# Half of a tile's edge messages added in pairs by VectorE, row scatters moved to the end of a step: a graph layer and an expert layer in one stream

## The chip, the cores and the metric

The kernel runs on one core of one Trainium2 chip. The metric is device time in microseconds of one launch, the median of several runs. A profile of one further execution gives the engines' instructions: PE is TensorE, DVE VectorE, ACT ScalarE, POOL GpSimd, SP SyncE. L12 is line 12 of the kernel.

## The reference, cut to what matters

Four layers on 6250 nodes with 256 features and 100000 edges: a first graph layer, a first expert layer, and then the two that matter here, a graph attention layer (4 heads of 64) and a layer of 8 experts, of which each node takes two.

```python
# third layer, x normalised per row
h = (x @ W).reshape(n, HEADS, OUT_C)
a_src = einsum('nhc,hc->nh', h, att_src); a_dst = einsum('nhc,hc->nh', h, att_dst)
e = a_src[src] + a_dst[dst]                 # edges, and a loop at each node
e = where(e > 0, e, 0.2 * e)
ex = exp(e - segment_max(e, dst)[dst])
alpha = ex / (segment_sum(ex, dst)[dst] + 1e-16)
out = segment_sum(alpha[:, :, None] * h[src], dst)
x = x + relu(out.reshape(n, 256) + bias)
# fourth layer, xf = x normalised again
gate_logits = xf @ Wg + bg                  # 8 experts
top_w, top_i = top_k(gate_logits, 2); top_w = softmax(top_w)
x = x + sum over the two experts e of top_w * (gelu(xf @ W1[e] + b1[e]) @ W2[e] + b2[e])
```

## The kernel before

Nodes are sorted by degree, so that a tile of 128 nodes has nodes of like degree; 49 tiles, and CAPS[t] is the number K of edge slots that tile t has (41, then 25 down to 8; 813 in all). A table in HBM holds for each node its row of h with its attention terms and, in the second half, x.

The third and fourth layers run as one stream (ffn1, from L1421), a loop of steps written out by hand: each engine runs its instructions in the order in which the program issues them. In step s

- POOL gathers tile s (gather, L1223): one indirect DMA for the tile's own rows (L1229), and one for each of its K slots (L1239), 128 rows each. The slots lie in one to four chunks of up to 13 slots, in buffers g of which there are five. After each gather the program calls between(), which issues one instruction from a list, the outbox, if there is one.
- DVE works on tile s-1 (q1): scores (L1247) and, after an exponential on ACT, shares (L1265), which writes the weights into PSUM. messages (L1276) multiplies the gathered rows of a chunk by their weights, in place (L1284). total (L1286) sums them over the slots on PE: one matmul with the identity for each slot, accumulated in PSUM (L1293; the fp32 matmul counts as two in the profile).
- Tile s-2 (q2) is finished: result (L1295) adds bias, relu and x, the row is normalised (L1547), turned by PE (L1550), and PE computes its gate logits (L1447). DVE adds the gate bias into sc (L1583).
- When a group of mostly four tiles has its logits, choose (L697), count (L732, on PE), place (L740) and listed (L793) find for each row its two experts and its two places in the experts' lists, and written (L825) has PE turn the list of full blocks (L830). The rows are then scattered to the experts' table, one indirect DMA of POOL for each tile and choice (scatters, L761; L768): for a group of four tiles 8 of them go into the outbox for the next step. Their offsets are the slots that place computes; the profile shows that wait under L802, an instruction of DVE just behind.
- One block of 256 rows is put through its expert per step, in three stages over three steps: rows and weights are fetched by SP (fetch, L1450, with xr at L844, which waits for the scatters of its round; fetch2, L1457); inner (L1463, matmuls L1470, gelu L1474); outer (L1476, L1481); and finish (L897, L899) on DVE. ACT normalises the fetched rows (L1489).

PE's order in a step is: outer, the turn of tile s-2, inner, the turn of the new block's rows, gate, total of chunk 0, count, total of the other chunks, written. DVE's order is: scores, result and normalisation, shares, messages of chunk 0, finish, choose, gate bias, places, messages of the other chunks, place and listed. Tiles come mostly in order of rising K, tile 0 with K = 41 in step 8. After the last tile the remaining blocks go through their experts alone, and the two parts of the output are added.

Of the kernel before, what the change touches and what calls it, by code (L numbers as in the profile page):

```python
# [27 lines left out]
CAPS = [41, 25, 24, 23, 22, 21, 21, 20, 20, 20, 19, 19, 19, 18, 18, 18, 18, 18, 17, 17, 17, 17, 16, 16,  # L28
        16, 16, 16, 15, 15, 15, 15, 15, 14, 14, 14, 14, 14, 13, 13, 13, 12, 12, 12, 12, 11, 11, 10, 9, 8]
# [6 lines left out]
def gnn_moe_kernel(ctx: ExitStack, tc: tile.TileContext, a: dict, out: bass.AP):  # L36
    nc = tc.nc
    x, src, dst = a["x"], a["src"], a["dst"]
    N, D = x.shape
# [28 lines left out]
    ident = keep.tile([P, P], F32, name="ident")  # L68
# [1207 lines left out]
    def messages(q, c):  # L1276

        al, own = q["al"], q["own"]
        if c == 0:
            hv = own[:, :D].rearrange("p (h c) -> p h c", h=H)  # L1280
            nc.vector.tensor_mul(hv, hv, al[:, q["K"], :, None].to_broadcast([P, H, C]))
        g, k0, m = q["gs"][c]
        gv = g[:, :m, :D].rearrange("p k (h c) -> p k h c", h=H)
        nc.vector.tensor_mul(gv, gv, al[:, k0 : k0 + m, :, None].to_broadcast([P, m, H, C]))  # L1284

    def total(sums, q, c):  # L1286

        po = sums[:, q["half"], :]
        if c == 0:
            nc.tensor.matmul(po, ident, q["own"][:, :D], start=True, stop=False)  # L1290
        g, k0, m = q["gs"][c]
        for k in range(m):
            nc.tensor.matmul(po, ident, g[:, k, :D], start=False, stop=k0 + k == q["K"] - 1)  # L1293

    def result(pool, sums, bias_b, q, x3):  # L1295
        y = pool.tile([P, D], F32, name="att_y")
# [124 lines left out]
    def ffn1(tab, bias_b):  # L1421
        NX, _, HD = a["L1_ffn_W1"].shape
        NM = HD // P
        with tc.tile_pool(name="f1", bufs=1) as fp, tc.tile_pool(name="f1r", bufs=2) as rp, \
# [7 lines left out]
            bg = fp.tile([P, NX], F32, name="bg")  # L1432
# [5 lines left out]
            with tc.tile_pool(name="f1p", bufs=2, space=PSUM) as psum:  # L1438
# [5 lines left out]
                def gate(xT):  # L1444
                    pl = small[:, 256 : 256 + NX]
                    for k in range(2):
                        nc.tensor.matmul(pl[:, :NX], xT[:, k, :], wg[:, k, :], start=(k == 0), stop=(k == 1))  # L1447
                    return pl
# [47 lines left out]
                seq = []  # L1496
                rows_in = 0
                for g, n in parts:
                    grp = dict(g=g, n=n, last=(g, n) == parts[-1], pad=g + n == NT)
# [9 lines left out]
                outbox, sends, coming, kept = [], [], [], []  # L1509
# [9 lines left out]
                s = 0  # L1519
                while s < len(seq) or ready or new or cur or prev or q1 or q2 or group or outbox or coming or kept:  # L1520
# [11 lines left out]
                    if q2 is not None:  # L1532
                        grp, i = q2["grp"], q2["i"]
# [22 lines left out]
                    if n_c:  # L1556
                        messages(q1, 0)
# [19 lines left out]
                    if q2 is not None:  # L1577
                        pl = gate(xT)
                    if group is not None:
                        st = moe.choose(rp, group["g"], group["n"], group["rw"], group["sc"], group["pad"])  # L1580
                        moe.weigh(st)
                    if q2 is not None:
                        nc.vector.tensor_add(grp["sc"][:, i, :], pl[:, :NX], bg)  # L1583
                    if n_c:
                        total(sums, q1, 0)
                    if group is not None:
# [4 lines left out]
                    for c in range(1, n_c):  # L1591
                        messages(q1, c)
                        total(sums, q1, c)
                    if group is not None:
                        slot = moe.place(rp, st)
                        moe.listed(rp, group["last"])
                        moe.compare(group["due"], group["last"])
                        li = moe.written(rp, psum)
                        if group["last"]:
                            nc.vector.tensor_copy(list_i, li)  # L1600
                            moe.left(left_i)

                    def between():
                        if outbox:
                            outbox.pop(0)()

                    q0 = None
                    if s < len(seq):
                        grp0, i0, end0 = seq[s]
                        q0 = gather(ap_, tab, grp0["g"] + i0, between)  # L1610
                        q0.update(grp=grp0, i=i0, end=end0, half=s % 2)
                    while outbox:
                        nc.gpsimd.memset(gap, 0.0)
                        between()
                    ready, coming = ready + coming, []
                    outbox, sends = sends, []
                    if group is not None:
# [6 lines left out]
                    q1, q2 = q0, q1  # L1624
# [3 lines left out]
        with tc.tile_pool(name="f1o", bufs=8) as op_, \  # L1628
# [21 lines left out]
            while ys:  # L1650
                g, n, k, y = ys.pop(0)
# [69 lines left out]
    with tc.tile_pool(name="order", bufs=1) as order_pool, \  # L1721
            tc.tile_pool(name="order_ps", bufs=1, space=PSUM) as order_psum:
        with tc.manual_schedule(engines={ET.SP, ET.PE, ET.Activation, ET.DVE, ET.Pool}), \
                tc.tile_pool(name="g1w", bufs=1) as g1w:
            with tc.tile_pool(name="f0", bufs=1) as fp:
                k0 = {"g1w": g1w}
# [7 lines left out]
    nc.vector.tensor_scalar_mul(bias_b, bias_b, fast)  # L1734
    whole.__exit__(None, None, None)
    ffn1(tab, bias_b)


# [27 lines left out]
```

## Time and profile before

| | us |
| --- | --- |
| median of 3 runs | 2492.31 (2491.33 to 2493.85) |
| profiled execution: own time | 2483.9 |
| profiled execution: span | 2482.2 |
| busy: PE / DVE / ACT / POOL | 1848.9 / 1219.9 / 941.8 / 1498.1 |
| first and last gather of the stream (L1239) start at | 828.6 and 2079.2 |
| last matmul of the experts (L1481) begins in the group at | 2409.99 |
| mean granted TensorE clock | 0.87 of full |

The span runs from the first to the last instruction. "issue" is idle time in which the engine waited for nothing that the profile shows. A group of instructions is shown with its line, engine, operation, output and inputs, its count, its busy time in us and the mean of one in ns, and the idle time of its engine just before it with what ended most of that. In a timeline the columns are the start in us, the duration in us, the engine, the line, and in brackets the idle time before with what ended it. Busy time of an engine alone does not say what bounds the kernel: PE, for instance, waits inside the stream while the sum of its work is the largest.

### The profile page before, as it was taken

The numbers are of one execution on the slowest core, as the hardware profiler recorded it, in microseconds if no ns is written. First come the engines' busy times: TensorE is split into PE (matmuls) and PEld (weight loads), VectorE is DVE, ScalarE is ACT, GpSimd is POOL, SyncE is SP. The second block draws the span as 40 slices with busy tenths as digits, with TensorE's granted clock in tenths as the row PEclk, the third lists the DMA queues.
The fourth block names the chain that finished last, engine by engine and source line by source line (L and its number), as shares of the span: only waits on it lengthen the run. The fifth ranks groups of instructions, "written<-read, shape, count | busy, mean of one in ns | idle before, by whom it ended". The sixth has DMA issues, their size and how long they took to land.

```text
span 2482.2 us, 31090 instructions
## 1 busy us (share of the span) xinstructions
PE 1848.9 (74%) x8343; PEld 1544.8 (62%) x8344; DVE 1219.9 (49%) x4459; ACT 941.8 (38%) x1967; POOL 1498.1 (60%) x1778
## 2 busy tenths in 40 slices
PE   4743758887967463549589898988989796799990
PEld 3522646676855342438478787777877676678880
DVE  3668765562328453455455564554646364311112
ACT  3754545553437220124234343343334232244330
POOL 3557357767545577676776767677777775234430
PEclk8955878898989776669899999999999998899995
DMA  7514345678869543355667667666766664387748
GB/s 215 122 40 132 108 140 169 198 222 236 255 201 297 134 115 104 99 175 156 209 206 223 205 192 220 214 204 203 237 200 201 198 199 157 115 290 262 266 170 312
DMA packets 346252, 471.68 MB, mean 190 GB/s; under 512 B 70206, under 2 KB 283237, under 8 KB 346071
## 3 DMA queue, kind: packets, MB, share of 16 engines
q1 hardware_dynamic: 261868, 272.15, 35.0%
q0 software_dynamic: 72112, 186.44, 25.4%
q10 hardware_dynamic: 12090, 11.03, 1.3%
q8 instruction: 69, 1.13, 0.2%
q14 instruction: 113, 0.92, 0.1%
HBM read 374.44 MB, written 95.02 MB: 189 GB/s over the span
## 4 chain that ended last, share of the span: by engine, by line
PE 33%; POOL 15%; DMA 7%; issue 7%; ACT 6%; DVE 5%; SPq 1%; DVEq 0%; POOLq 0%; ACTq 0%
POOL g L1239 11%; PE ph L1470 10%; PE py L1481 10%; PE sums L1293 7%; DMA g<-t_d,idx 3%; POOL idx L253 2%; PE ph L1038 2%; DMA yg<-f_parts 2%; DMA idx<-src_d,start_i 1%; POOL f_rows L768 1%; ACT L1474 1%; ACT L402 1%; ACT hT L1474 1%; ACT bxn L1489 1%; ACT L1263 1%
## 5 line engine op out<-in xcount | busy, mean ns | idle before, releaser
L1239 POOL DMA_INDIRECT g<-t_d,idx x813 | 776.4, 955 | 248.6 <-issue 228.2
L1470 PE MATMUL ph<-bxT,w 128*128 128x256 f32 x1728 | 411.4, 395 | 29.7 <-ACT hT L1474 29.7
L1470 PEld LDWEIGHTS ph<-bxT,w 128*128 128x128 f32 x1728 | 337.8, 199 | 90.7 <-ACT hT L1474 43.8
L1293 PE MATMUL sums<-g,ident 128*128 128x256 f32 x1626 | 387.5, 398 | 2.8 <-DVE g L1284 2.8
L1481 PE MATMUL py<-w,hT 128*128 128x256 f32 x1728 | 386.0, 382 | 2.0 <-DMA w<-in_L_ffn_W 2.0
L1293 PEld LDWEIGHTS sums<-g,ident 128*128 128x128 f32 x1626 | 323.8, 201 | 59.9 <-DVE g L1284 12.4
L1481 PEld LDWEIGHTS py<-w,hT 128*128 128x128 f32 x1728 | 329.3, 192 | 47.0 <-DMA w<-in_L_ffn_W 2.3
L768 POOL DMA_INDIRECT f_rows<-rw,slot x196 | 197.9, 1010 | 134.3 <-DVE ci L802 71.6
L1284 DVE TENSOR_TENSOR g<-g,weights 128x2048 f32<-128x2048 f32 (+6 forms) x88 | 229.5, 2610 | 0.0
L1474 ACT ACTIVATE hT<-ph,bcol 128x256 f32<-128x256 f32 x432 | 177.3, 471 | 136.5 <-PE ph L1470 131.1
L897 DVE SCALAR_TENSOR_TENSOR by<-ob,bw,by 128x256 f32<-128x256 f32 x216 | 97.9, 480 | 263.0 <-ACT by L892 263.0
L1263 ACT ACT_TABLE_LOAD x36 | 46.2, 1283 | 442.5 <-DVE lg L1262 314.5
L903 POOL DMA_INDIRECT f_parts<-by,btok x108 | 106.2, 984 | 147.2 <-DVE by L897 101.7
L1550 PE MATMUL pT<-ident,xn 128*128 128x128 f32 x98 | 25.1, 347 | 225.8 <-DVE xn L1547 225.8
L1550 PEld LDWEIGHTS pT<-ident,xn 128*128 128x128 f32 x98 | 13.3, 169 | 239.0 <-issue 230.7
L1254 DVE TENSOR_TENSOR lg<-g,own 128x32 f32<-128x32 f32 (+6 forms) x88 | 16.7, 196 | 292.2 <-DMA g<-t_d,idx 243.8
L892 ACT ACTIVATE by<-py,bw 128x256 f32<-128x256 f32 x216 | 92.4, 472 | 158.6 <-PE py L1481 124.8
L1041 ACT ACTIVATE h<-ph,bcol 128x256 f32<-128x256 f32 x216 | 90.5, 470 | 155.8 <-PE ph L1038 94.0
L903 POOL DMA_INDIRECT f_parts<-by,toks x44 | 42.2, 959 | 163.0 <-DVE by L899 124.3
L446 PE MATMUL proj<-we,xT 128*128 128x264 f32 x392 | 106.7, 418 | 28.9 <-ACT xT L462 28.9
L1038 PE MATMUL ph<-bxT,w 128*128 128x256 f32 x432 | 108.2, 406 | 15.8 <-ACT bxT L864 14.6
L1038 PE MATMUL ph<-h,w 128*128 128x256 f32 x432 | 112.2, 419 | 0.6 <-ACT h L1041 0.6
(325 smaller groups left out, 2907.4 us busy)
## 6 DMA issues: line engine op xcount, KB each, us to landing
w<-in_L_ffn_W SPq DMA_DIRECT2D x108, 1024.0 KB
w<-in_L_ffn_expert_w SPq DMA_DIRECT2D x162, 256.0 KB
xr<-f_rows SPq DMA_DIRECT2D x108, 264.0 KB
yg<-f_parts SPq DMA_DIRECT2D x36, 512.0 KB
g<-t_d,idx POOLq DMA_INDIRECT x813
late_y<-by SPq DMA_DIRECT2D x64, 128.0 KB
late<-late_y SPq DMA_DIRECT2D x32, 256.0 KB
ob<-in_L_ffn_expert_b SPq DMA_DIRECT2D x54, 128.0 KB
```

What stands on the lines that cost most here:

```text
L446: nc.tensor.matmul(ph, xT[:, k, :], we[:, k, :], start=(k == 0), stop=(k == 1))
L768: put = nc.gpsimd.indirect_dma_start(out=self.table[:, :], out_offset=bass.IndirectOffsetOnAxis(ap=slot[:np_, c, i : i + 1], axis=0), in_= ...
L892: nc.scalar.activation(y, py, AF.Copy, scale=b["w"][:, i : i + 1])
L897: nc.vector.scalar_tensor_tensor(y, b["ob"], w, y, op0=OP.mult, op1=OP.add)
L903: put = nc.gpsimd.indirect_dma_start(out=self.parts[:, :], out_offset=bass.IndirectOffsetOnAxis(ap=tok, axis=0), in_=y, in_offset=None,)
L1038: nc.tensor.matmul(ph[:, m, :], b["ws"][i][:, k, m * P : (m + 1) * P], hi[:, k, :], start=(k == 0), stop=(k == 1))
L1239: nc.gpsimd.indirect_dma_start(out=g[:, k, :], out_offset=None, in_=halves(tab), in_offset=bass.IndirectOffsetOnAxis(ap=idx[:, o : o + 1], ...
L1284: nc.vector.tensor_mul(gv, gv, al[:, k0 : k0 + m, :, None].to_broadcast([P, m, H, C]))
L1293: nc.tensor.matmul(po, ident, g[:, k, :D], start=False, stop=k0 + k == q["K"] - 1)
L1470: nc.tensor.matmul(ph[:, q, :], b["w1"][:, k, m * P : (m + 1) * P], b["xT"][:, k, :], start=(k == 0), stop=(k == 1))
L1474: nc.scalar.activation(hT[:, m, :], ph[:, q, :], AF.Gelu, bias=b["bcol"][:, m : m + 1])
L1481: nc.tensor.matmul(py, b["hT"][:, m, i * P : (i + 1) * P], b["w2"][:, m, :], start=(m == 0), stop=(m == NM - 1))
```

## The change

Three edits, all in the stream.

1. messages: after the multiplication of a chunk of m slots, DVE adds the last m // 2 slots onto the first m // 2, in place, in one instruction. total then sums only the first m - m // 2 slots on PE. Of the 813 slots 384 are added by DVE.
2. between(): it issues from the outbox only when the gathers left in the step are fewer than the entries left in the outbox, so that the outbox goes between the last gathers of the step in place of the first. Steps without gathers empty it as before (force).
3. DVE's addition of the gate bias into sc moves from before total of chunk 0 to behind the messages and totals of the other chunks.

```diff
         nc.vector.tensor_mul(gv, gv, al[:, k0 : k0 + m, :, None].to_broadcast([P, m, H, C]))
+        u = m // 2
+        nc.vector.tensor_add(g[:, :u, :D], g[:, :u, :D], g[:, m - u : m, :D])
...
-        for k in range(m):
-            nc.tensor.matmul(po, ident, g[:, k, :D], start=False, stop=k0 + k == q["K"] - 1)
+        u = m - m // 2
+        for k in range(u):
+            nc.tensor.matmul(po, ident, g[:, k, :D], start=False, stop=c == len(q["gs"]) - 1 and k == u - 1)
...
-                    if q2 is not None:
-                        nc.vector.tensor_add(grp["sc"][:, i, :], pl[:, :NX], bg)
                     if n_c:
                         total(sums, q1, 0)
...
                     for c in range(1, n_c):
                         messages(q1, c)
                         total(sums, q1, c)
+                    if q2 is not None:
+                        nc.vector.tensor_add(grp["sc"][:, i, :], pl[:, :NX], bg)
...
+                    calls = CAPS[seq[s][0]["g"] + seq[s][1]] if s < len(seq) else 0
+
-                    def between():
-                        if outbox:
+                    def between(force=False):
+                        nonlocal calls
+                        calls -= 1
+                        if outbox and (force or calls < len(outbox)):
                             outbox.pop(0)()
...
                     while outbox:
                         nc.gpsimd.memset(gap, 0.0)
-                        between()
+                        between(True)
```

## The prediction

> **What bounds the kernel now.** I read the groups of the page first, then POOL's waits between 828 and 2170 us (the stream of gathers and the start of its tail), then POOL's timeline, and last the stretches where POOL and DVE meet. Times are those of the profiled execution: span 2482.2 us, own time 2483.9 us (1.7 us lie around the span). The median of the timed runs, 2492.31 us, is 8.4 us above it; I work out a difference in the profile and put it on the median.
>
> ```profile
> L1239 POOL DMA_INDIRECT g<-t_d,idx x813 | 776.4, 955 | 248.6 <-issue 228.2
> L1293 PE MATMUL sums<-g,ident 128*128 128x256 f32 x1626 | 387.5, 398 | 2.8 <-DVE g L1284 2.8
> L1284 DVE TENSOR_TENSOR g<-g,weights 128x2048 f32<-128x2048 f32 (+6 forms) x88 | 229.5, 2610 | 0.0
> ```
>
> The reader is to see 813 gathers of 0.955 us with 0.3 us of "issue" before each, and 1626 matmuls (two per edge slot) that almost never wait for DVE.
>
> ```profile
> POOL g L1239 <- issue: 228.2, 749, 0.3
> POOL f_rows L768 <- DVE ci L802: 71.6, 11, 10.9
> ...
> POOL g L1239 <- PE sums L1293: 6.7, 19, 1.2
> ```
>
> Columns: who waited for whom, total us, times, longest. POOL's gathers hardly ever wait for a buffer that PE has to free (1.2 us at most); it waits at length only at row scatters, for the slots that DVE computes.
>
> ```profile
> 1459.16 0.94 POOL L1229 DMA_INDIRECT own<-t_d,node_i  x1 [0.30 <-issue]
> 1460.41 0.95 POOL L1239 DMA_INDIRECT g<-t_d,idx  x1 [0.30 <-issue]
> 1469.59 0.98 POOL L768 DMA_INDIRECT f_rows<-rw,slot  x1 [8.23 <-DVE ci L802]
> 1470.87 0.97 POOL L1239 DMA_INDIRECT g<-t_d,idx  x1 [0.30 <-issue]
> ```
>
> This is the start of step 28: own row, one gather, then 8.2 us of nothing. The stream is POOL's. From 828.6 to 2080.4 us (1251.8 us) POOL has 952 instructions, busy 911.9 us; with 951 gaps of 0.30 us that is 1197 us, and nearly all the rest is such waits. At K = 16 PE needs 23.45 us a step (py 1424.16 to py 1447.61). POOL needs 17 x 1.25 = 21.25, plus a quarter of 8 scatters of 1.28 = 2.6, plus about 2 of waits: 25.8. PE is close behind, but POOL ends last, and PE idles for it (17.2 us just before the last step).
>
> **The change, part by part.**
>
> Sums. Of 813 slots 384 leave PE: 768 matmuls of 0.2155 us (32 in 6.9 us), 165 us of PE. PE's step at K = 16 falls to 20.0 us. POOL does not wait for it, so in the stream this is worth nothing by itself; it only brings the slots somewhat earlier.
>
> Adds. 88 adds of u x 256 elements, both inputs in SBUF. The nearest rows are L1654 (128x1024, 1.226 us) and L1203 (128x512, 0.691 us): 1.045 ns an element, so u = 3, 4, 5, 6 (15, 38, 23, 12 times) take 0.96, 1.22, 1.49, 1.76 us, 116 us in all. DVE is busy 639 of the stream's 1252 us, so it stays at 60% and does not become the bound. But there is a second price, on POOL:
>
> ```profile
> 781.88 0.69 DVE L1203 TENSOR_TENSOR x_all<-x_all,yg 128x512 f32<-128x512 f32 x1
> ...
> 782.15 1.24 POOL L253 DMA_INDIRECT idx<-src_d,start_i  x1 [0.30 <-issue]
> ...
> 783.70 0.95 POOL L253 DMA_INDIRECT idx<-src_d,start_i  x1 [0.31 <-issue]
> ```
>
> ```profile
> 238.43 2.61 DVE L195 TENSOR_TENSOR hot<-iota_f,kind 128x2352 bf16<-128x2352 f32 x1
> ...
> 239.06 2.81 POOL L768 DMA_INDIRECT f_rows<-rw,slot  x1 [0.22 <-issue]
> ```
>
> An indirect DMA that starts while DVE adds two SBUF tensors takes longer, by exactly the time from 0.12 us after its own start to the end of the DVE instruction: 782.57 - 782.27 = 0.30 (measured 1.24 - 0.95), 241.04 - 239.18 = 1.86 (measured 1.85). The multiply L1284, whose weights lie in PSUM, does nothing of the kind: 160 gathers that had at least 0.3 us of it beside them average 0.950. And a DVE instruction that began less than about 0.2 us before that point does not hold the gather (1432.94: 0.95 us, beside an L899 begun at 1432.84). So an add of length D holds POOL over h = D - 0.2. With a gather point every 1.25 us and any phase, the mean delay is h x h / 2.5 up to h = 1.25, and h - 0.625 above: 0.23, 0.42, 0.67, 0.93 us for the four sizes. For the 86 adds beside the stream (the last tile's two come after it) that is 3.4 + 15.9 + 15.3 + 9.3 = 44 us. Laid on the traced gathers right behind each L1284, shifted by 0 to 1.2 us, they would cost 36 to 46. Bounds: 0 if no add holds POOL, 95 if each holds it for its whole h. I take 44.
>
> The Trainium skill, page "SBUF — State Buffer", section "Who interferes with whom", states that a DVE instruction with two SBUF inputs contends with a GpSimd instruction that reads SBUF, and that whichever began first keeps the other out until it is done; by that rule the trace agrees (0.30 and 1.85 us above).
>
> Scatters. In the stream POOL's waits for slots were 1.52, 10.71, 9.81, 3.66, 10.39, 8.23, 5.75 and 1.78 us, and one gather waited 1.25 for PE: less 0.30 each, 50.4 us. Now the 8 scatters go between the last 8 gathers, the first one (K - 6) x 1.25 us after the step's start: 8.75 us at K = 13, 10 at 14, 12.5 at 16, 13.75 at 17. The slots were ready 12.9, 12.1, 12.6 and 10.4 us after those starts; with the other steps under 8. At most 4.2 + 2.1 + 0.1 us stay; the slot also comes some 2 us sooner (half the sums before the count matmuls, no stall of DVE at the gate), so I leave 1 us. Number and length of POOL's instructions stay. What waits behind the moved scatters: the row fetch on SP (L844), which waits for them to land, and w1 and w2 behind it. The scatters now end with the step's last gather, some 3 us before the next step's scores; the rows are wanted by ACT (L1489) 10 us after those scores and w2 a step later. Cover about 7 us; if it fails, PE slips in one step of four, and PE now has some 4 us a step to spare.
>
> Gate bias. DVE stood 169 us at L1583 for PE's gate, ahead of the later messages; that stall goes, but DVE's wait for gathers is what follows it. Nothing on POOL: 0.
>
> Tail. After the last gather the last tile's sums lose 24 matmuls (5.2 us), but PE's next work is the list transposes (L830), which wait for DVE's placing, and that now stands behind two adds of 1.76 us. In that step I get 0.7 us. From 2111 us on nothing changes.
>
> Sum: -50.4 + 1 + 44 - 0.7 = -6 us. Profile 2483.9 to about 2478; median 2492.3 to **2486 us**.
>
> **Rivals.**
>
> A, the forecast: the stalls at the scatters go and the adds give nearly as much back, gather by gather. With the add cost at 30 to 58 us it ends at 2472 to 2500. Chance 0.69.
>
> B, the adds pass POOL by, because their long strided reads leave it room, or because they fall mostly where POOL is in its gap: -50 us, 2442. For it: many L897 and L899 in the stream cost nothing (66 of each, 5 us together). Against it: the two rows above, to a hundredth. Chance 0.13. The same section of the skill infers that descriptor generation needs only the write interface, so that a tensor_tensor leaves a DMA from POOL alone; the 1.24 us above speak against that here.
>
> C, slower: DVE's adds are tied in phase to the gathers that release them (scores start at a landing), and each meets a gather near the start of its hold. At the full h the price is 95 us: -50 + 95 = +45, 2537 us. It turns slower from 0.58 us per add on, and I forecast 0.51. For it: 0.07 us is all that lies between. Against it: the shifted phases above all give under 46. Chance 0.16, of which a third lies below 2508.
>
> D, PE sets the stream after all: up to -165 us, 2327. Against it: POOL's table of waits. Chance 0.02. That the scatters do not really move is part of A's bound (6 us).
>
> **Numbers.** Range 2462 to 2508: all of A, a third of C, a corner of B. About 0.2% (5 us) is what a measurement of this kernel can tell from no change. Within A (spread about 8 us around -6) I put 0.55 under -5, 0.35 within, 0.10 above. Faster 0.38 + 0.13 + 0.02 = 0.53; same 0.24 and a little of C, 0.26; slower the rest, 0.21.
>
> **What will show it.** Right: POOL's wait for L802 in the stream near zero; mean gather up from 955 to about 1000 ns, the long ones each ending with an add; last gather within 10 us of 2079; PE idle before L1550 larger. Wrong: gathers still at 955 (B), or at 1050 and more (C), a row fetch that ACT or PE waits for, or new waits of POOL for PE or DVE.

## The result, and the profile after

The changed kernel takes 2478.3 us (median of 6 runs, 2472.3 to 2482.3) where the kernel before takes 2492.3 (6 runs, 2487.7 to 2495.0): a ratio of 0.9944, interval 0.9929 to 0.996, or 14 us less. The forecast was 6 us less. Some of the runs told of below were made under conditions in which every kernel, the one before too (3328 us), took a third longer; a time is compared only with that of the kernel before timed beside it.

The page of the changed kernel, the groups that answer to the three shown of before, and the new add (L1296 is the old L1293, L1286 the add):

```profile
L1239 POOL DMA_INDIRECT g<-t_d,idx x813 | 819.2, 1008 | 247.7 <-issue 228.5
...
L1296 PE MATMUL sums<-g,ident 128*128 128x256 f32 x858 | 230.8, 427 | 36.6 <-DVE g L1286 36.5
...
L1284 DVE TENSOR_TENSOR g<-g,weights 128x2048 f32<-128x2048 f32 (+6 forms) x88 | 229.8, 2611 | 0.0
...
L1286 DVE TENSOR_TENSOR g<-g 128x1024 f32<-128x1024 f32 (+3 forms) x88 | 116.5, 1324 | 3.0
```

The same 813 gathers now take 1.008 us each in place of 0.955, 43 us more in all. The multiplies are unchanged, the adds take the 116 us that the rows of before gave, and PE has 858 sum matmuls in place of 1626 and begins to wait for DVE (36.5 us in place of 2.8). POOL's waits in the changed kernel, in the same stretch as shown of before (828 to 2170 us):

```profile
POOL g L1239 <- issue: 228.5, 750, 0.3
...
POOL f_rows L768 <- DVE ci L802: 20.0, 3, 9.6
...
POOL g L1239 <- PE sums L1296: 3.0, 10, 0.3
```

Of the 20.0 us at the scatters 18.1 fall after the last gather (9.55 and 8.50); in the stream one wait of 1.98 us is left, in the step with K = 13. So POOL lost its stalls and got longer gathers. Where a single gather got longer shows in its timeline beside DVE's, around two adds of five slots each:

```profile
1823.69 1.49 DVE L1286 TENSOR_TENSOR g<-g 128x1280 f32<-128x1280 f32 x1
1823.77 2.23 POOL L1239 DMA_INDIRECT g<-t_d,idx  x1 [0.30 <-issue]
...
1830.98 1.49 DVE L1286 TENSOR_TENSOR g<-g 128x1280 f32<-128x1280 f32 x1
1831.36 1.92 POOL L1239 DMA_INDIRECT g<-t_d,idx  x1 [0.30 <-issue]
```

By the rule of the prediction a gather's point is 0.12 us after its start. The first gather reaches it at 1823.89 and the add ends at 1825.18: 1.29 us; it took 1.28 longer than 0.95. The second: 1832.47 - 1831.48 = 0.99, and it took 0.97 longer. Over the whole stream 70 of 86 adds met an instruction of POOL in this way; the rule of the prediction gives 44.6 us for them, the records 43.9.

### The profile page after: what moved, and what is told of

Its sections match the earlier page's. It is cut to its first block, busy times and chain, and to the rows that moved or that the text cites. A ratio compares the mean times of both kernels' runs of the same rounds, so it can differ in the third digit from the quotient of the medians.

```text
span 2480.4 us, 29632 instructions
## 1 busy us (share of the span) xinstructions
PE 1727.2 (70%) x7575; PEld 1427.0 (58%) x7576; DVE 1339.9 (54%) x4547; ACT 942.7 (38%) x1967; POOL 1544.7 (62%) x1778
## 4 chain that ended last, share of the span: by engine, by line
POOL 21%; PE 19%; DMA 11%; issue 9%; DVE 9%; ACT 4%; SPq 0%; DVEq 0%; POOLq 0%; ACTq 0%
POOL g L1239 15%; PE ph L1473 7%; PE py L1484 7%; DMA g<-t_d,idx 6%; POOL f_rows L768 3%; DVE g L1284 2%; POOL idx L253 2%; DMA yg<-f_parts 2%; PE ph L1038 2%; PE sums L1296 2%; DMA idx<-src_d,start_i 1%; ACT L402 1%; ACT L1263 1%; DVE g L1286 1%; POOL own L1229 1%
## 5 line engine op out<-in xcount | busy, mean ns | idle before, releaser
L1239 POOL DMA_INDIRECT g<-t_d,idx x813 | 819.2, 1008 | 247.7 <-issue 228.5
L1473 PE MATMUL ph<-bxT,w 128*128 128x256 f32 x1728 | 433.5, 411 | 22.2 <-ACT hT L1477 22.1
L1473 PEld LDWEIGHTS ph<-bxT,w 128*128 128x128 f32 x1728 | 355.5, 209 | 88.6 <-ACT hT L1477 34.6
L1484 PE MATMUL py<-w,hT 128*128 128x256 f32 x1728 | 393.9, 387 | 0.8 <-DMA w<-in_L_ffn_W 0.8
L1484 PEld LDWEIGHTS py<-w,hT 128*128 128x128 f32 x1728 | 335.1, 195 | 48.3 <-DMA w<-in_L_ffn_W 1.0
L1296 PE MATMUL sums<-g,ident 128*128 128x256 f32 x858 | 230.8, 427 | 36.6 <-DVE g L1286 36.5
L897 DVE SCALAR_TENSOR_TENSOR by<-ob,bw,by 128x256 f32<-128x256 f32 x216 | 98.0, 480 | 247.1 <-ACT by L892 246.9
L1296 PEld LDWEIGHTS sums<-g,ident 128*128 128x128 f32 x858 | 182.7, 216 | 77.7 <-DVE g L1286 48.4
L1038 PE MATMUL ph<-bxT,w 128*128 128x256 f32 x432 | 108.7, 407 | 15.1 <-ACT bxT L864 13.3
L1286 DVE TENSOR_TENSOR g<-g 128x1024 f32<-128x1024 f32 (+3 forms) x88 | 116.5, 1324 | 3.0
```

Source lines behind the costliest of these rows:

```text
L897: nc.vector.scalar_tensor_tensor(y, b["ob"], w, y, op0=OP.mult, op1=OP.add)
L1038: nc.tensor.matmul(ph[:, m, :], b["ws"][i][:, k, m * P : (m + 1) * P], hi[:, k, :], start=(k == 0), stop=(k == 1))
L1239: nc.gpsimd.indirect_dma_start(out=g[:, k, :], out_offset=None, in_=halves(tab), in_offset=bass.IndirectOffsetOnAxis(ap=idx[:, o : o + 1], ...
L1286: nc.vector.tensor_add(g[:, :u, :D], g[:, :u, :D], g[:, m - u : m, :D])
L1296: nc.tensor.matmul(po, ident, g[:, k, :D], start=False, stop=c == len(q["gs"]) - 1 and k == u - 1)
L1473: nc.tensor.matmul(ph[:, q, :], b["w1"][:, k, m * P : (m + 1) * P], b["xT"][:, k, :], start=(k == 0), stop=(k == 1))
```

## The experiments

The theory: POOL bounds the stream; its stalls at the scatters were some 50 us, and adds with both operands in SBUF hold its gathers for 40 to 45 us. Rival B: the adds cost POOL nothing. Rival D: PE sets the stream.

**Without the adds** (edits 2 and 3 of the change, all slots summed by PE).

```diff
-        u = m // 2
-        nc.vector.tensor_add(g[:, :u, :D], g[:, :u, :D], g[:, m - u : m, :D])
```

> The change without its adds: the scatters at the end of the step and the gate bias behind the messages, all 813 slots summed by PE. Theory (an add of two SBUF tensors holds POOL's gathers for 44 us in all, the stalls at the scatters were 50 us): mean gather back to 955 ns, waits for L802 in the stream under 5 us, last gather about 50 us sooner than before, median near 2442 us. Rival B (adds cost POOL nothing): no faster than the change itself, 2478 us. Rival D (PE sets the stream): slower than the change by up to 165 us, since PE has its 768 matmuls back.

Measured: 2450.9 us against 2492.2, ratio 0.9831 (0.9814 to 0.9848), and 28 us faster than the change (2479.1, timed beside it). The gathers are back at their old length:

```profile
L1239 POOL DMA_INDIRECT g<-t_d,idx x813 | 775.9, 954 | 250.0 <-issue 226.1
```

B and D are out: leaving the adds away made the kernel faster, though PE has all its sums again. But it is 9 us short of the 2442. POOL's waits between 900 and 2040 us say where they went:

```profile
POOL f_rows L768 <- DVE ci L802: 11.2, 4, 6.1
POOL g L1239 <- PE sums L1293: 8.7, 21, 2.6
```

With PE's full sums the scatters got their slots only 14.6, 13.1, 11.4 and 13.6 us after the start of the steps with K = 13, 14, 15 and 16, so that four still waited, and one gather waited 2.6 us for a buffer (the other waits in that line are the usual gaps of 0.3 us).

**The adds alone** (edit 1; scatters and gate bias where they were).

> The adds alone, scatters and gate bias where they were. Theory: mean gather near 1005 ns (44 us more on POOL), stalls at the scatters shorter by about 2 us each because the slots come sooner (about 35 of 50 us left), so 25 to 40 us slower than before: 2517 to 2532 us. Rival B: 15 us faster than before, 2477 us. Rival D: up to 165 us faster.

Measured: 2528.9 us against 2492.2, ratio 1.015 (1.0132 to 1.0167), 37 us slower: inside what the theory gave, against both rivals. The mean gather is near the 1005 ns expected:

```profile
L1239 POOL DMA_INDIRECT g<-t_d,idx x813 | 811.4, 998 | 247.7 <-issue 228.2
```

One part of the expectation failed: the stalls at the scatters did not shrink to 35 us (50.0 in the stream). They fell in some steps (K = 13: 5.9 us in place of 10.7) and grew in others (K = 16: 12.6 in place of 10.4). PE's waits between 900 and 2100 us suggest why the slots came no sooner on the whole:

```profile
PE pT L1553 <- DVE xn L1550: 215.8, 29, 44.4
PE sums L1296 <- DVE g L1286: 100.1, 45, 3.3
```

With DVE still stalled at the gate before the later messages, PE now stands at each later chunk until its add is done. The matmuls behind such a wait also took longer: in one step 8 of them took 3.56 us after a wait of 1.87 (from 1379.06 us), and 8 without a wait 1.89 (from 1374.72); what slows them was not followed. In the change itself, where the gate bias is behind the messages, the wait for adds is 28.6 us between 900 and 2040. The change has the scatters moved as well, and no run has edits 1 and 2 without edit 3: that the third edit pays only together with the first is argued, not shown.

**The same adds with one operand in PSUM.** The second operand is the weights, spread over the 64 features of a head. This kernel leaves half of the messages out of the sum, so its output is not the layer's; only its times are read.

```diff
-        nc.vector.tensor_add(g[:, :u, :D], g[:, :u, :D], g[:, m - u : m, :D])
+        hv = gv[:, :u]
+        nc.vector.tensor_add(hv, hv, al[:, k0 : k0 + u, :, None].to_broadcast([P, u, H, C]))
```

> The change with its adds kept in number and length, but the second operand is the weights, which lie in PSUM, in place of the other half of the messages; the other half is left out of the sum. Theory (two SBUF inputs are what holds POOL): adds of the same 1.2 us, mean gather back to about 955 ns, median near 2442 us. Rival (DVE's time, or the halved sums, make the gathers longer, whatever the operands): mean gather stays near 1008 ns, median near 2478 us.

Measured: 2440.6 us against 2492.2, ratio 0.979 (0.9775 to 0.9806). The adds are as many and as long (first line, DVE's groups), and the gathers are back at their old length (second, the page):

```profile
L1287 DVE TENSOR_TENSOR g<-g,weights 128x1024 f32<-128x1024 f32 (+3 forms) x88 | 115.9, 1317 | 3.0
```

```profile
L1239 POOL DMA_INDIRECT g<-t_d,idx x813 | 776.5, 955 | 249.0 <-issue 228.5
```

By the rule of the prediction these adds would have cost POOL 41.3 us at the 70 places where one met POOL's point; the records there show 0.3 us. What holds POOL is the second operand in SBUF, not DVE's time and not the halved sums. That the new operand is also a spread one is no rival: in the profile of before a multiply by such an operand in SBUF (L595, from 234.15 to 234.84 us) met a scatter that began at 234.32 and took 1.35 us, some 0.4 longer than the others, and 0.40 us lie between the scatter's point and the multiply's end. The Trainium skill, page "SBUF — State Buffer", section "Who interferes with whom", infers that a tensor_tensor leaves descriptor generation alone; its other rule, two SBUF inputs against an instruction of POOL that reads SBUF, is the one that these 41.3 and 0.3 us bear out.

This run against the one without adds also prices the halved sums where no add holds POOL: stream 1203.1 against 1211.5 us (first to last gather), medians 10 us apart. Most of that lies at the scatters, which with the halved sums got their slots sooner: one stall of 3.2 us in the stream, where the run without adds has 11.2.

**The change once more**, for a second profile.

> The changed kernel once more, timed in five rounds beside the one before, with a second profile. The two profiles differ by 5 us between the stream's start and the end, the medians by 14 us. If the 14 us are the change's, this ratio is near 0.9944 again and a second profile ends some 10 us sooner; if they are partly the scatter of the runs, the ratio is nearer 0.9975 (6 us).

Measured: 2479.1 us against 2492.2, ratio 0.9945 (0.9931 to 0.9958). The 14 us are the change's. The other half of the expectation failed: the second profile ends at 2479.6 us, only 0.8 sooner than the first, and the missing time must be sought in the profile of before. In this second profile 69 adds met POOL and cost 41.6 us.

**The kernel before once more**, for a second profile: before_again fell to the 3330 us conditions, before2 did not.

> The kernel before once more, for a second profile and for the scatter of runs. In the first profile the stream's first gather began at 828.6 us, in four later profiles of other kernels, whose code up to there is the same, at 832 to 836. If the first profile was an early one only up to the stream, this one has its first gather near 834 us, a stream of 1251 us and a span near 2489 us; if its stream was short too, the stream here is some 1258 us.

Measured there: 3332.0 us against 3328.4; its first gather at 1084 us tells nothing about the question. Inconclusive.

> The kernel before once more, as before_again, for a second profile. If the first profile was early only up to the stream, this one has its first gather near 834 us, a stream of 1251 us and a span near 2489 us; if its stream was short too, the stream here is some 1258 us.

Measured: span 2494.8 us, first gather at 834.3, stream 1257.5, tail 403.0. The first profile was early in both parts: 5.7 us before the stream, 6.9 in it. The stream's 6.9 us are the stalls: 58.6 us here at eight scatters, where the first profile had 51.9.

```profile
POOL f_rows L768 <- DVE ci L802: 78.5, 10, 11.3
```

(Of these 78.5 us, 19.9 lie after the last gather.) From the first gather to the end the two profiles of before take 1653.6 and 1660.5 us, those of the change 1648.4 and 1644.5.

**Two scatters between each of the last four gathers**, on top of the kernel without adds, against the four waits seen there.

```diff
-                        if outbox and (force or calls < len(outbox)):
+                        if outbox and (force or 2 * calls < len(outbox)):
                             outbox.pop(0)()
+                            if outbox and not force:
+                                nc.gpsimd.memset(gap, 0.0)
+                                outbox.pop(0)()
```

> No adds, gate bias behind the messages, and the scatters two at a time between the last four gathers of a step (a small memset of POOL between two). The slots came 14.6, 13.1, 11.4 and 13.6 us after the step's start in the run without the adds; the first scatter now stands 13.8 us (K = 13) and 15 us or later (K = 14 and more) after it. Theory: the 11 us of stalls there go to about 1, 2441 us. Rival: the scatters now land after the row fetch is wanted, and PE slips: 2451 us or more.

Measured there: 3324.4 us against 3328.4, ratio 0.9988 (0.9972 to 1.0004). Inconclusive for its question; POOL waited 571 us for PE in that run.

> The kernel of pairs once more (no adds, gate bias behind the messages, two scatters between each of the last four gathers), because in the call of pairs all kernels, the one before too, took some 3330 us with ACT standing idle some 16 us in every step. Theory, where the kernel before takes about 2492 us: the 11 us of stalls at the scatters of the run without the adds go to about 1: 2441 us. Rival: the rows land too late for their fetch and PE slips, 2451 us or more.

Measured: 2448.7 us against 2496.4, ratio 0.9805 (0.9792 to 0.9818). That is neither the 2441 of the theory nor the 2451 of the rival. The stalls at the scatters went, as the theory had it, to 0.8 us, and about half of what they had cost came back as something neither side named:

```profile
POOL g L1239 <- PE sums L1293: 14.9, 20, 4.6
```

In the steps with K = 14 PE, with all its sums, needs some 22.6 us (23.45 less four matmuls) and POOL 18.75 and, on the mean, 2.6 for scatters; POOL, no longer stalled, runs into its five buffers and waits for PE (4.6 and 3.3 us in two steps; 0.3 of each is its usual gap). The late scatters did no harm: in the stream PE never waits for a fetched row.

**Gate bias alone, and scatters alone**, under the same 3330 us conditions.

> The gate bias behind the messages, alone. Theory: POOL bounds the stream, so only what makes slots come sooner counts: the stalls at the scatters shrink by 0 to 1.5 us each, 2480 to 2492 us. Rival: DVE's stall at the gate (169 us) is on the path, and a good part of it is gained: under 2470 us.

> The scatters moved to the step's last gathers, alone; gate bias and sums as before. Theory: most of the 50 us of stalls go; what stays is 10 us or a little more than in the run without the adds (11 us at the scatters), because DVE still stalls at the gate before the slots: 2450 to 2456 us. Rival (the later scatters make the row fetch late, and PE with it): waits of ACT or PE for xr, and no better than 2470 us.

Measured: 3333.9 and 3325.7 us against 3328.4, ratios 1.0019 (1.0008 to 1.0029) and 0.9997 (0.9983 to 1.0011). In before_again ACT stood idle 306 us in 21 waits ahead of L1552 (31.5 at most), which the trace puts down to another core or an unknown queue; PE waited for ACT, and POOL for PE (378 us). So POOL did not bound the stream there, and shorter stalls at its scatters could gain little. Neither edit was tried alone under the conditions of the forecast. That the scatters' move pays there is shown with the gate bias only (no_adds).

**The add cut into single slots.**

```diff
-        nc.vector.tensor_add(g[:, :u, :D], g[:, :u, :D], g[:, m - u : m, :D])
+        for k in range(u):
+            nc.vector.tensor_add(g[:, k, :D], g[:, k, :D], g[:, m - u + k, :D])
```

> The change with each chunk's add cut into u adds of one slot (128x256), one right behind the other; outputs unchanged. If the hold is each instruction's own (0.42 us less 0.2, so 0.02 us of delay each, 384 of them), the adds cost POOL about 8 us in place of 41: median near 2445 us, mean gather near 960 ns. If adds one behind the other hold POOL through (four L897 in a row held a gather for 1.12 us in the profile of before), each train of 1.2 to 2.5 us holds like one long add: 60 to 82 us, median 2495 to 2520 us, mean gather 1020 to 1045 ns.

**Multiplies and adds in turn**, slot by slot: the second half multiplied first, then for each slot of the first half its multiply (weights in PSUM) and its add.

> The change with the chunk's second half multiplied first, and then, slot by slot, the multiply of a slot of the first half (weights in PSUM) and its add; outputs unchanged. Between two adds there is always an instruction with one operand in PSUM. Theory: POOL gets in at the next such instruction, so 384 adds of 0.42 us cost 0.02 to 0.03 us each, 8 to 12 us: stream near 1213 us, median 2446 to 2452 us; DVE has some 140 us more to do and stays under 65% in the stream. Rival (DVE's chain now makes the slots and sums late): waits of POOL for L802 or for PE come back, 2460 us or more.

Both ran under the 3330 us conditions: 3208.7 us (ratio to before 0.9629, 0.959 to 0.9668) and 3233.0 (0.9709, 0.9667 to 0.975). The expected times can't be read there, but the holds can, gather by gather. An example of split, four adds in 1.43 us and the gather that meets them:

```profile
2143.26 1.43 DVE L1287 TENSOR_TENSOR g<-g 128x256 f32<-128x256 f32 x4
...
2143.65 1.19 POOL L1239 DMA_INDIRECT g<-t_d,idx  x1 [0.30 <-issue]
...
2145.14 0.94 POOL L1239 DMA_INDIRECT g<-t_d,idx  x1 [0.30 <-issue]
```

Held to the end of the four, to 2144.69, the gather would have taken 0.92 us longer; it took 0.24, which is the end of the add that was running. At 63 places where such a train met POOL the holds come to 8.5 us; each instruction holding for itself gives 8.0, the whole train 54.6. Mean gather 964 ns in split, 962 in woven (whose holds were not counted one by one). So the hold is the single add's, and between two short adds POOL gets in. That does not hold for every train: the expectation of split names four L897 in a row, with two operands in SBUF too, in the profile of before (397.61 to 399.26 us). The gather L568 that met them at 398.05 took 2.07 us: it was held to the end of the last of the four. Why POOL got in between the adds and not there is open. That split gains 120 us under these conditions fits its 768 matmuls less (165 us of PE) where POOL waits for PE; no run parts that from its other edits.

## Why the prediction was right, step by step

**What bounds.** Right: POOL. Without the adds PE has nearly twice the sum matmuls, and the kernel is 28 us faster than the change.

**Adds.** Forecast 44 us on POOL, measured 43.9 and 41.6 in the change's two profiles, 35.9 in the adds alone (61 places). The mechanism is shown by the pair of 41.3 and 0.3 us above.

**Scatters.** Mechanism right, size taken from one execution: 50.4 us of stalls in the first profile, 57.7 by the same count in the second (58.6 less 0.3 for each of eight, and 1.5 at a gather). What stays was forecast at 1 us and is 1.7. The slot was to come some 2 us sooner; with K = 14 and 16 it came about 5 and 6 us sooner.

**Sums.** "In the stream this is worth nothing by itself" is the step that was wrong, though the sum did not need it: once the scatters are moved and nothing holds POOL, the halved sums are worth 8 to 10 us (psum_add against no_adds). Without them the slots come too late for the moved scatters in four steps, and where the scatters stand later still, POOL waits for PE (pairs2). PE also gave up less than the forecast 165 us: L1293 was busy for 387.5, L1296 is for 230.8, which is 157 less, and a sum matmul takes 427 ns on the mean in place of 398.

**Gate bias.** Forecast 0. By itself nothing shows a gain. PE's wait for the adds is 100 us with the adds alone and 29 us in the change, which the forecast did not look at; how much of that is the gate bias and how much the moved scatters no run tells.

**Tail.** Forecast 0.7 us, measured 1.9 and 2.5 (403.0 to 401.1 and 400.5). Of the 5.2 us of the 24 matmuls some 2 were gained; PE waits 2.1 us for an add in the tail of the first profile, as forecast, and the rest was not followed.

**The sum.** In the profile it was made from: forecast -6, measured 1653.6 to 1648.4, -5.2 from the first gather on. The medians' -14 are the difference of the means of two profiles each, 1657.1 and 1646.5, that is -10.6, and some 3 us that these profiles do not show; the forecast fell short in part because its one profile had short stalls. The net is a small difference of two terms near 50 us, and the range was 46 us wide: that the median fell inside it says little, and the measured gain is more than twice the forecast. What bears the prediction out are the two terms, each measured by itself.

**Rivals.** B is refuted by psum_add and no_adds. C's price (95 us) did not come: 70 and 69 of 86 adds met POOL, at 0.51 and 0.48 us for the mean add, where 0.51 was forecast for any phase. D is refuted.

## What to carry to other kernels

When one engine issues without a pause, ask of each instruction given to another engine what it does to that one's own duration: here the right place to look was the length of single gathers beside DVE's instructions, by operand, in a part of the trace far from the change. Work taken off an engine that is not the bound can still pay: it sets how far the bound can be relieved before that engine holds it up. And a stretch read from one profile is one draw: the stalls that were to be gained differed by 7 us between two executions of the same kernel.

## What the hardware showed that was not expected

The hold needs an add that began a little before the gather's point, 0.12 us after the gather's start. In the run with the adds alone the first gather below came to its point 0.18 us into an add and was held to its end; the second came 0.14 us into one and was not held:

```profile
1123.06 1.76 DVE L1286 TENSOR_TENSOR g<-g 128x1536 f32<-128x1536 f32 x1
1123.12 2.52 POOL L1239 DMA_INDIRECT g<-t_d,idx  x1 [0.30 <-DVE g L1284]
...
1330.46 1.27 DVE L1286 TENSOR_TENSOR g<-g 128x1024 f32<-128x1024 f32 x1
1330.48 0.95 POOL L1239 DMA_INDIRECT g<-t_d,idx  x1 [0.30 <-DVE g L1284]
```

So for these adds the limit lies between 0.14 and 0.18 us; the prediction's 0.2 rests on an L899 that began 0.22 us before such a point and held nothing. In a train of short adds the hold ends with the add that began it (63 places, 8.5 us against 54.6); in the train of four L897 it lasted to the end of the train.

Under the 3330 us conditions ACT stood idle although its operand was written: in before_again, for one, from 1699.1 to 1715.1 us, though PE had written the operand of L1552 by 1704.3. The trace puts these waits down to another core or an unknown queue. The runs at 3330 us were on other chips (2 and 7) than those at 2490 us whose chip is on record (11 and 14); whether that is the cause was not tried.
